# One buffer pool for the weights of an attention stack, and weight splits that wait for DVE's low parts

## The chip, the cores and the metric

The kernel runs on one core of a Trainium2 chip. The metric is device time of one launch in microseconds, the median of several runs. Profiles come from one execution that the hardware profiler recorded.

## The reference

Two transformer-like layers over 2 × 1024 rows of 512 (a residual stream `x`), all float32. Layer 0 adds to `x` a single-head attention of width 128 and a mixing of four streams of 128 columns, whose 4 × 4 matrix per row comes out of 50 Sinkhorn steps. Layer 1 adds a causal attention and an expert layer:

```python
q = (hidden_states @ Wq.T).reshape(b, s, H, D)          # H = 32 heads, D = 128
k = (k_cmp @ Wk_up.T).reshape(b, s, HK, D)              # HK = 8, from a latent of 256 + 256
v = (v_cmp @ Wv_up.T).reshape(b, s, HK, D)
attn = softmax(where(causal, q @ k.T * scale, -1e9))
out = (attn @ v) @ Wo.T                                 # plus a gated LoRA feed-forward of 8 experts
```

Both layers work on a layer-normed `x`. Layer 1 is 2 batches of 1024 rows, and each has 8 groups of four heads that share a key and a value head.

## The kernel before

**Precision.** Every matmul is made of three passes on float16 pairs: a value is split into a high part and a low part (the rest), and high × high, high × low and low × high are summed. So every operand has to be split, by ScalarE (high) and VectorE (low) for results, by GpSimd for weights: `split_pool` is three GpSimd instructions on 128 × 512 (L94 scales in place, L95 writes the high part, L96 subtracts for the low part).

**Layer 1 attention (`layer1_attn`)** walks 16 groups (2 batches of 8) and in each 32 slots. In slot `s` of a group, `row_step` makes one row block: 32 query rows of four heads (128 partitions) against 32·(s+1) keys. PE computes the scores (L88, tile `s`); DVE takes the row minimum of the negated scores with the mask (L282, L286); ACT the exponential (L290) and, one slot later, the scaled high part (`rows_hi`, L307); DVE the low part (`rows_lo`, L313); SP's queue transposes both by DMA to `PT` (L318). A width that is no multiple of 128 is padded with zeros by a GpSimd memset (L317). `last_row` holds the last row minimum recorded so far.

Around the rows other work is recorded at fixed slots by `at(g, s, f)`: attention times values (`av`, L343) from slot `4c + 2k + 5`, output projections (`wo_block`, its result added by DVE at L729) from `4c + 10`, query projections of the next group from 18 or 19, keys and values of the next group (`kv`) from slot 1. Weights are fetched on GpSimd's queue (`fetch`, L677, into the four `f2k` buffers) and then split by `parts_of`. The slots before:

- key and value weights of group g+1: fetched at slot 1, split at 3 (at the end of a batch 17 and 19)
- query weights: fetched at 5, 9, 13, 17, split at 7, 11, 15, 19
- output weights: fetched at 33, 35, 37, 39, split at 35, 37, 39, 41, which are slots 1 to 9 of the next group

**Buffers.** Key and value weights go to a pool `h2k` of three buffers, output weights to `wo` of five, query weights to `wq` of four; all are 2 KB per partition. `h2k` and `wo` also take the normed tiles on their way to the transposed `xT` (`normed_T`), the tiles of the second batch's gate (`tile_of`) and latent weights (`lat_w`).

**Order.** Each engine's queue is in order. The order of each is made when the program is built: a list scheduler places instructions by modelled times and the dependencies that were recorded. `behind(i, j)` adds a dependency without a semaphore: i is placed after j in the modelled order, and nothing waits at run time. In `parts_of` the first instruction of a split is put behind `last_row` in this way. `tc.issue_after(i)` orders the instructions of a block that run on i's engine behind i.

**Other work in the groups.** Recorded at slots of the first eight groups: the Sinkhorn steps of the second batch (`chain_step`, DVE reciprocals L542 and L547 between GpSimd sums L537 to L545), the mixing (`mix0_units`, GpSimd L629), gates, a second layer norm, expert weights (`ffn_w`, which calls `split_pool` directly into `cmp`), and the latent weights.

Of the kernel before, what the change touches and what calls it, by code (L numbers as in the profile page):

```python
# [9 lines left out]
F16 = mybir.dt.float16  # L10
# [6 lines left out]
P = 128  # L17
S = 1024
NB = 2
NT = S // P  # L20
H = 512
NC = H // P
# [3 lines left out]
CAPACITY = 768.0  # L26
LN_EPS = 1e-5
RMS_EPS = 1.1920929e-07
FB, HB, PB, LB, XB, WB = 4, 3, 3, 3, 4, 5
QR = 32  # L30
NR = P // QR
LG = ((0, 1, 2, 3), (4, 5, 6, 7))
# [19 lines left out]
def tile_model(ctx: ExitStack, tc: tile.TileContext, out: bass.AP, a: dict):  # L52
# [11 lines left out]
    def T(tag, shape, dt=F32, bufs=None):  # L64
        count[0] += 1
        kw = {} if bufs is None else {"bufs": bufs}
        return sb.tile(shape, dt, tag=tag, name=f"{tag}_{count[0]}", **kw)

    def C(name, shape, dt=F32):
        return const.tile(shape, dt, tag=name, name=name)  # L70
# [109 lines left out]


    last_pool, last_row, last_T = [None], [None], [None]
    last_hi, last_lo = [None], [None]

    def after(*insts):

# [2 lines left out]
            st.enter_context(tc.issue_after(i.ins))  # L189
        return st  # L190

    def behind(i, j):

        tc.add_manual_dep(i.ins, j.ins.name, mybir.DependencyInfo(
            mybir.DependencyClass.NoSync, mybir.DependencyReason.DATA), reason="behind")

    def rsqrt(y, ve, tag):

# [24 lines left out]
        return V.scalar_tensor_tensor(rs[:, 1, sl], mv[:, sl, 0], -1.0, rs[:, 2, sl],  # L223
                                      ALU.mult, ALU.mult)

    def normed_T(b, mv, rs, t, dst, pool, tags=(("f2k", FB), ("h2k", HB))):

        xn = T(tags[0][0], [P, NC, P], bufs=tags[0][1])
        xf = xn.rearrange("p c d -> p (c d)")
        hl = T(tags[1][0], [P, NC, 2, P], F16, bufs=tags[1][1])  # L230
        if pool > 1:
            A.activation(xf, acc[b, t], AF.Identity, scale=rs[:, 2, t:t + 1], bias=rs[:, 1, t:t + 1])
        elif pool:
            G.tensor_scalar(xf, acc[b, t], rs[:, 2, t:t + 1], rs[:, 1, t:t + 1], ALU.mult, ALU.add)
        else:
            V.tensor_scalar(xf, acc[b, t], rs[:, 2, t:t + 1], rs[:, 1, t:t + 1], ALU.mult, ALU.add)
        last_hi[0] = A.activation(hl[:, :, 0, :], xn, AF.Copy)
        eng = G if pool in (1, 2) else V
        lo = eng.tensor_tensor(hl[:, :, 1, :], xn, hl[:, :, 0, :], ALU.subtract)
        (last_pool if eng is G else last_lo)[0] = lo  # L240
        last_T[0] = nc.sync.dma_start_transpose(dst, hl.rearrange("p c l d -> p (c l d)"))
# [67 lines left out]
    def rows_lo(Pm, r, W, pool, hl, dst):  # L309
        if pool:  # L310
            G.tensor_tensor(hl[:, 1, :W], Pm[:, :W], hl[:, 0, :W], ALU.subtract)
        else:
            lo = V.scalar_tensor_tensor(hl[:, 1, :W], Pm[:, :W], r[:, 1:2], hl[:, 0, :W],  # L313
                                        ALU.mult, ALU.subtract)
        if W < hl.shape[2]:

            behind(G.memset(hl[:, :, W:], 0.0), lo)  # L317
        nc.sync.dma_start_transpose(dst, hl.rearrange("p l k -> p (l k)"))  # L318
# [32 lines left out]
    def front0(b, between=lambda: None):  # L351
        mv, rs = layernorm(b, "a")
        xT = T("xT", [P, NT, 2 * NC, P], F16, bufs=1)
        for ts in F0[b]:
            layernorm_tiles(b, mv, rs, ts)
            for t in ts:
                if b == 0:
                    tags = ("wq", 4), (("h2k", HB), ("wo", WB))[t % 2]
                    normed_T(b, mv, rs, t, xT[:, t], FP[b][t], tags)
                    if t == X1:  # L360
                        with tc.issue_after(last_T[0].ins):
                            load_x(1)
                else:
                    normed_T(b, mv, rs, t, xT[:, t], FP[b][t])
                    between()
            if b == 0 and ts[0] == 0:
                split_w0a()
        lead = [x[0] for x in (last_pool, last_hi, last_lo)]

        ms = T("rms", [P, NT], bufs=2)  # L370
        V.tensor_tensor(ms, rs[:, 0], rs[:, 0], ALU.mult)
        V.tensor_tensor(ms, ms, mv[:, :, 1], ALU.mult)
        V.tensor_scalar(ms, ms, RMS_EPS, None, ALU.add)
        rf = T("rf", [P, NT], bufs=2)
        rsqrt(rf, ms, "rs")
        V.tensor_scalar(rf, rf, 1.0 / 1024.0, None, ALU.mult)
        lg = C(f"lg{b}", [P, NT, 24])
        Vh = T("V", [P, NT, 2, P], F16, bufs=2)
        for t in range(NT):
            p = PP() if t % 2 or b else srow()  # L380
            mm3(p[:, :152], [(lambda l, c=c: xT[:, t, 2 * c + l, :],
                              lambda r, c=c: wv0[:, c, r, :]) for c in range(NC)])
            V.scalar_tensor_tensor(lg[:, t, :], p[:, 128:152], rf[:, t:t + 1], base24,
                                   ALU.mult, ALU.add)
            if CV[b]:
                vf = T("y", [P, P], bufs=1)
                A.activation(vf, p[:, 0:128], AF.Copy)
                A.activation(Vh[:, t, 0, :], vf, AF.Copy)
                G.tensor_tensor(Vh[:, t, 1, :], vf, Vh[:, t, 0, :], ALU.subtract)
            else:  # L390
                evac(p[:, 0:128], Vh[:, t, 0, :], Vh[:, t, 1, :], 1.0)
            between()
        logit[b] = lg

        hh = C(f"hh{b}", [P, NT, 2, 4])
        l4 = lg[:, :, 16:24].rearrange("p t (k n) -> p t k n", k=2)
        mx = T("hmx", [P, NT, 2], bufs=1)
        V.tensor_reduce(mx, l4, AX.X, ALU.max)
        V.tensor_tensor(hh, l4, bc(mx, 3, 4), ALU.subtract)
        A.activation(hh, hh, AF.Exp)  # L400
        V.tensor_reduce(mx, hh, AX.X, ALU.add)
        V.reciprocal(mx, mx)
        V.tensor_tensor(hh, hh, bc(mx, 3, 4), ALU.mult)

        V.tensor_scalar(hh[:, :, 1, :], hh[:, :, 1, :], 1.0 / 128.0, None, ALU.mult)
        if b == 0:
            with after(*lead):
                split_w0b()
        Q = T("Q", [P, 2, S], F16, bufs=2)
        K = T("K", [P, 2, S], F16, bufs=2)  # L410
        for half in range(2):
            sl = slice(512 * half, 512 * half + 512)
            for k, dst in ((0, Q), (1, K)):
                p = proj_T(lambda c, l: wqk0[:, c, l, k * P:(k + 1) * P], xT, half)
                if CQ[b]:
                    qf = T("f2k", [P, 512], bufs=FB)
                    A.activation(qf, p, AF.Identity, bias=bqkv[:, k:k + 1])
                    A.activation(dst[:, 0, sl], qf, AF.Copy)
                    G.tensor_tensor(dst[:, 1, sl], qf, dst[:, 0, sl], ALU.subtract)
                    continue  # L420
                A.activation(dst[:, 0, sl], p, AF.Identity, bias=bqkv[:, k:k + 1])
                V.scalar_tensor_tensor(dst[:, 1, sl], p, bqkv[:, k:k + 1],
                                       dst[:, 0, sl], ALU.add, ALU.subtract)
        return Q, K, Vh, xT, hh, rs
# [243 lines left out]
    def lat_w(mc):  # L668
        st = T("f2k", [P, NC, P], bufs=FB)
        nc.gpsimd.dma_start(st, a["Wlat"][mc])  # L670
        w1 = T("h2k", [P, 2, NC, P], F16, bufs=HB)
        split_pool(st, w1[:, 0], w1[:, 1], 32.0)
        return w1

# [4 lines left out]

    def parts_of(st, tag, scale, bufs):  # L680

        hl = T(tag, [P, 2, 512], F16, bufs=bufs)
        behind(split_pool(st, hl[:, 0], hl[:, 1], scale), last_row[0])
        return hl

    def kv(b, g):
# [4 lines left out]
            got["st"] = fetch(a["Wup"][g])  # L691

        def split():
            w = parts_of(got["st"], *(("h2k", 32.0, HB) if g + b else ("wo", 32.0, WB)))
            got["w"] = w.rearrange("p l (s c d) -> p l s c d", s=2, c=2)
            got["K"] = T("K", [P, 2, S], F16, bufs=2)
            got["V"] = T("V", [P, 2, NT, P], F16, bufs=2)
# [60 lines left out]
    def layer1_attn(kv0, start, extra):  # L758
# [5 lines left out]
        def at(g, s, f):  # L764
            g, s = g + s // NS, s % NS
            fill.setdefault((g, s), []).append(f)
# [29 lines left out]
        for g in range(N):  # L796
            if g + 1 < N:
# [8 lines left out]
                for u in range(4):  # L806
                    at(g, QNN + 2 * u if new else QN + 4 * u, lambda g=g, u=u: q_unit(g + 1, u))
                for hh in range(4):
                    at(g, 33 + 2 * hh, lambda g=g, hh=hh: fetch_wo(g + 1, hh))
                    at(g, 35 + 2 * hh, lambda g=g, hh=hh: split_wo(g + 1, hh))  # L810
            for u in range(4):
                at(g, QH + (1 if (g + 1) % NG == 0 else 3) * u, lambda g=g, u=u: q_unit(g, 4 + u))
            for c in range(NT):
# [174 lines left out]
        xT1[b] = T("xT", [P, NT, 2 * NC, P], F16, bufs=1)  # L988

    def xT_tile(b, t, pool):  # L990
        normed_T(b, *ln1[b], t, xT1[b][:, t], pool, (("f2k", FB), ("h2k", HB)) if b else
                 (("xr", XB), (("h2k", HB), ("wo", WB))[t % 2]))

    def tile_of(b, t):
        d = T("h2k", [P, 2 * NC, P], F16, bufs=HB)
        normed_T(b, *ln1[b], t, d, True, (("f2k", FB), ("xr", XB)))
        return d

# [36 lines left out]
        extra.setdefault((s // (S // QR), s % (S // QR)), []).append(f)  # L1035

    def chain_step():
        with tc.issue_after(last_row[0].ins):
            next(chain, None)

    for k in range(102):
# [93 lines left out]
```

## Time and profile before

| | |
|---|---|
| Median of 3 runs | 1868.62 us (1867.13 to 1870.87) |
| Profiled execution | 1873.71 us |
| Its span | 1871.6 us |
| Granted TensorE clock, mean | 0.971 |
| VectorE busy | 1473.9 us (79%) |
| GpSimd busy | 900.4 us (48%) |
| DMA | 230.25 MB, mean 123 GB/s |

PE is TensorE, PEld its weight loads, DVE VectorE, ACT ScalarE, POOL GpSimd, SP SyncE. Busy times are per engine, so they overlap. Layer 0 ends at about 234 us; a group of layer 1 takes about 92 us. In a row such as `out<-in`, the names are the program's tiles. Idle time in brackets behind an instruction is its engine's, with what ended it.

### The profile page before, as it was taken

What the parts mean: (1) busy time and instruction counts of PE and PEld (TensorE: products, weight loads), DVE (VectorE), ACT (ScalarE), POOL (GpSimd) and SP (SyncE); (2) the same over time, 40 slices, a digit from 0 to 9 for tenths busy, and PEclk for the clock granted to TensorE, in tenths of its full rate; (3) what the DMA queues carried; (4) which work ended last, traced back from release to release, by engine and by line L of the source; (5) the groups of instructions that cost most, each with busy time, mean ns of one, the idle gap of its engine ahead of it and who ended that gap; (6) DMA issues with size and microseconds to landing.
All of it is one profiled execution on the core that took longest, in us unless ns stands there. A gap on an engine that the chain in (4) does not pass through costs nothing. (4 is left out here: it accounts for less than half of the span.)

```text
span 1871.6 us, 34948 instructions
## 1 busy us (share of the span) xinstructions
PE 1724.0 (92%) x11458; PEld 1047.7 (56%) x11458; DVE 1473.9 (79%) x4050; ACT 1198.8 (64%) x2917; POOL 900.4 (48%) x1540
## 2 busy tenths in 40 slices
PE   4756399989999999999999999999999999999998
PEld 3333145656666566566555556566666666655665
DVE  8888977988888878787967767777777878777675
ACT  4747665657666787867535646666676767675554
POOL 5657667576857373727525332334242415155200
PEclk9887699999999999999999999999999999999999
DMA  7425234656554656477538645756565666666456
GB/s 209 91 46 112 76 66 96 149 113 133 129 127 104 150 121 152 99 146 159 134 85 154 124 101 128 131 125 146 115 143 123 137 123 141 118 143 138 89 125 119
DMA packets 707305, 230.25 MB, mean 123 GB/s; under 512 B 689953, under 2 KB 690081, under 8 KB 707122
## 3 DMA queue, kind: packets, MB, share of 16 engines
q1 hardware_dynamic: 691666, 180.75, 47.2%
q0 software_dynamic: 13152, 43.07, 8.6%
q10 hardware_dynamic: 2304, 4.20, 0.7%
q8 instruction: 90, 1.47, 0.3%
q14 instruction: 93, 0.76, 0.1%
HBM read 52.81 MB, written 4.19 MB: 30 GB/s over the span
## 5 line engine op out<-in xcount | busy, mean ns | idle before, releaser
L290 ACT ACTIVATE P<-P,nm 128x1024 f32<-128x1024 f32 (+31 forms) x528 | 391.7, 742 | 261.3 <-DVE nm L282 248.3
L313 DVE SCALAR_TENSOR_TENSOR Phl<-P,r,Phl 128x1024 f16<-128x1024 f32 (+31 forms) x515 | 464.5, 913 | 109.5 <-ACT Phl L307 104.6
L343 PE MATMUL av<-PT,V 128*128 128x256 f16 x3648 | 451.9, 275 | 18.3 <-DMA PT<-Phl 12.7
L88 PE MATMUL s<-K,Q 128*128 128x512 f16 (+22 forms) x2400 | 447.3, 319 | 22.0 <-DVE P L286 16.0
L343 PEld LDWEIGHTS <-V 128*128 128x128 f16 x3648 | 357.6, 99 | 110.4 <-issue 11.6
L307 ACT ACTIVATE Phl<-P,r 128x1024 f16<-128x1024 f32 (+31 forms) x515 | 370.2, 732 | 28.7 <-DMA PT<-Phl 12.6
L88 PE MATMUL pp<-wo,ao 128*128 128x512 f16 x1536 | 373.7, 380 | 4.6 <-ACT ao L104 3.7
L88 PE MATMUL pp<-xT,wq 128*128 128x512 f16 x1536 | 369.3, 380 | 0.9 <-DVE xr L855 0.5
L317 POOL MEMSET Phl<- 128x192 f16 (+2 forms) x384 | 75.8, 207 | 530.5 <-DMA PT<-Phl 414.1
L88 PEld LDWEIGHTS <-Q 128*128 128x128 f16 x2400 | 224.0, 99 | 180.6 <-issue 34.1
L88 PEld LDWEIGHTS <-wq 128*128 128x128 f16 x1536 | 149.6, 98 | 167.5 <-issue 3.0
L88 PEld LDWEIGHTS <-ao 128*128 128x128 f16 x1536 | 149.6, 98 | 155.6 <-ACT ao L104 5.6
L282 DVE CUSTOM_DVE_ANT_0 P<-s,mask,nm 128x272 f32<-128x272 f32 (+15 forms) x256 | 157.4, 616 | 21.2 <-PE s L88 13.3
L286 DVE TENSOR_SCALAR_CACHE_REDUCE P<-s 128x512 f32<-128x512 f32 (+15 forms) x272 | 152.4, 561 | 14.6 <-PE s L88 11.4
L302 ACT ACTIVATE r<-r 128x1 f32<-128x1 f32 x528 | 96.4, 193 | 76.2 <-DVE r L301 76.0
L104 ACT ACTIVATE ao<-av 128x512 f16<-128x512 f32 x128 | 75.4, 589 | 107.2 <-PE av L343 104.0
L301 DVE RECIPROCAL r<-r 128x1 f32<-128x1 f32 x528 | 80.7, 157 | 77.4 <-ACT P L290 73.2
L94 POOL TENSOR_SCALAR f2k<-f2k 128x512 f32<-128x512 f32 x164 | 110.3, 679 | 48.3 <-DMA f2k<-in_Wq 19.3
L729 DVE SCALAR_TENSOR_TENSOR acc<-pp,acc 128x512 f32<-128x512 f32 x128 | 86.8, 678 | 38.3 <-PE pp L88 37.9
L105 DVE SCALAR_TENSOR_TENSOR Q<-pp,Q 128x512 f16<-128x512 f32 x128 | 87.2, 681 | 31.9 <-ACT Q L104 31.8
L282 DVE CUSTOM_DVE_ANT_0 P<-s,mask 128x32 f32<-128x32 f32 (+15 forms) x256 | 104.9, 429 | 8.7 <-PE s L88 8.3
L104 ACT ACTIVATE Q<-pp 128x512 f16<-128x512 f32 x128 | 74.5, 582 | 55.1 <-PE pp L88 53.4
(262 smaller groups left out, 2113.5 us busy)
## 6 DMA issues: line engine op xcount, KB each, us to landing
f2k<-in_Wq POOLq DMA_DIRECT2D x64, 256.0 KB, 3.2
f2k<-in_WoT POOLq DMA_DIRECT2D x64, 256.0 KB, 3.3
PT<-Phl SPq DMA_TRANSPOSE x528, 3.4
acc<-in_x SPq DMA_DIRECT2D x16, 256.0 KB, 4.0
f2k<-in_Wup POOLq DMA_DIRECT2D x16, 256.0 KB, 3.6
out<-acc ACTq DMA_DIRECT2D x16, 256.0 KB, 3.7
xr<-in_x SPq DMA_DIRECT2D x12, 256.0 KB, 3.0
f2k<-in_Wlat POOLq DMA_DIRECT2D x8, 256.0 KB, 5.5
```

The source lines that it names most:

```text
L88: nc.tensor.matmul(dst, lhs(l), rhs(r), start=(i == 0 and j == 0), stop=(i == n - 1 and j == 2))
L94: first = G.tensor_scalar(stage, stage, scale, 1.0, ALU.mult, ALU.mult)
L104: A.activation(hl_hi, src, AF.Copy, scale=scale)
L105: return V.scalar_tensor_tensor(hl_lo, src, scale, hl_hi, ALU.mult, ALU.subtract)
L282: last_row[0] = V.tensor_tensor_reduce(Pm[:, o:o + w], pt[:, :w], mask[:, 512 - w:], -scale, first, ALU.add, ALU.min, nm[:, k:k + 1])
L286: last_row[0] = V.tensor_scalar(Pm[:, o:o + w], pt[:, :w], -scale, first, ALU.mult, ALU.min, accum_out=nm[:, k:k + 1])
L290: A.activation(Pm[:, :W], Pm[:, :W], AF.Exp, bias=last, scale=-1.0, accum_out=r[:, 0:1])
L302: A.activation(r[:, 1:2], r[:, 1:2], AF.Copy, scale=PSCALE)
L307: A.activation(hl[:, 0, :W], Pm[:, :W], AF.Copy, scale=r[:, 1:2])
L313: lo = V.scalar_tensor_tensor(hl[:, 1, :W], Pm[:, :W], r[:, 1:2], hl[:, 0, :W], ALU.mult, ALU.subtract)
L343: nc.tensor.matmul(p, Vh(j, l), PT(r * nj + j), start=(j == 0 and k == 0), stop=(j == nj - 1 and k == 2))
L729: V.scalar_tensor_tensor(acc[b, t], p, 1.0 / 256.0, acc[b, t], ALU.mult, ALU.add)
```

## The change

`h2k` is dropped: its users and those of `wo` share one pool `wo` of nine buffers. The logits of layer 0 move from one constant buffer per batch to one buffer for both. `behind` can make a dependency with a semaphore, and `parts_of` uses it: a split now waits at run time for `last_low`, the last low part (L313) that is recorded. The four output weights of group g+1 are split at slots 22, 25, 28, 31 of group g (26, 28, 30, 32 at the end of a batch), each fetched two slots earlier. The Sinkhorn steps of the second batch are put behind `last_low` instead of `last_row`, without a semaphore.

```diff
-FB, HB, PB, LB, XB, WB = 4, 3, 3, 3, 4, 5
+FB, PB, LB, XB, WB = 4, 3, 3, 4, 9
...
-    last_hi, last_lo = [None], [None]
+    last_hi, last_lo, last_low = [None], [None], [None]
...
-    def behind(i, j):
+    def behind(i, j, wait=False):
+        kind = mybir.DependencyClass.Sync if wait else mybir.DependencyClass.NoSync
         tc.add_manual_dep(i.ins, j.ins.name, mybir.DependencyInfo(
-            mybir.DependencyClass.NoSync, mybir.DependencyReason.DATA), reason="behind")
+            kind, mybir.DependencyReason.DATA), reason="behind")
...
             lo = V.scalar_tensor_tensor(hl[:, 1, :W], Pm[:, :W], r[:, 1:2], hl[:, 0, :W],
                                         ALU.mult, ALU.subtract)
+            last_low[0] = lo
...
-        lg = C(f"lg{b}", [P, NT, 24])
+        lg = T("lg", [P, NT, 24], bufs=1)
...
     def parts_of(st, tag, scale, bufs):
         hl = T(tag, [P, 2, 512], F16, bufs=bufs)
-        behind(split_pool(st, hl[:, 0], hl[:, 1], scale), last_row[0])
+        behind(split_pool(st, hl[:, 0], hl[:, 1], scale), last_low[0] or last_row[0], True)
...
-            w = parts_of(got["st"], *(("h2k", 32.0, HB) if g + b else ("wo", 32.0, WB)))
+            w = parts_of(got["st"], "wo", 32.0, WB)
...
                 for hh in range(4):
-                    at(g, 33 + 2 * hh, lambda g=g, hh=hh: fetch_wo(g + 1, hh))
-                    at(g, 35 + 2 * hh, lambda g=g, hh=hh: split_wo(g + 1, hh))
+                    s = 26 + 2 * hh if new else 22 + 3 * hh
+                    at(g, s - 2, lambda g=g, hh=hh: fetch_wo(g + 1, hh))
+                    at(g, s, lambda g=g, hh=hh: split_wo(g + 1, hh))
...
     def chain_step():
-        with tc.issue_after(last_row[0].ins):
+        with tc.issue_after(last_low[0].ins):
             next(chain, None)
```

The rest of the diff renames `h2k` to `wo` in `normed_T`, `front0`, `lat_w`, `xT_tile` and `tile_of`.

More of the change, by code (lines that the diff above doesn't have):

```diff
@@ L224, in layernorm_tiles, with normed_T @@
                                       ALU.mult, ALU.mult)
-    def normed_T(b, mv, rs, t, dst, pool, tags=(("f2k", FB), ("h2k", HB))):
+    def normed_T(b, mv, rs, t, dst, pool, tags=(("f2k", FB), ("wo", WB))):
         xn = T(tags[0][0], [P, NC, P], bufs=tags[0][1])
@@ L357, in front0 @@
                 if b == 0:
-                    tags = ("wq", 4), (("h2k", HB), ("wo", WB))[t % 2]
+                    tags = ("wq", 4), ("wo", WB)
                     normed_T(b, mv, rs, t, xT[:, t], FP[b][t], tags)
@@ L670, in lat_w @@
         nc.gpsimd.dma_start(st, a["Wlat"][mc])
-        w1 = T("h2k", [P, 2, NC, P], F16, bufs=HB)
+        w1 = T("wo", [P, 2, NC, P], F16, bufs=WB)
         split_pool(st, w1[:, 0], w1[:, 1], 32.0)
@@ L990, in xT_tile @@
     def xT_tile(b, t, pool):
-        normed_T(b, *ln1[b], t, xT1[b][:, t], pool, (("f2k", FB), ("h2k", HB)) if b else
-                 (("xr", XB), (("h2k", HB), ("wo", WB))[t % 2]))
+        normed_T(b, *ln1[b], t, xT1[b][:, t], pool, (("f2k", FB), ("wo", WB)) if b else
+                 (("xr", XB), ("wo", WB)))
     def tile_of(b, t):
-        d = T("h2k", [P, 2 * NC, P], F16, bufs=HB)
+        d = T("wo", [P, 2 * NC, P], F16, bufs=WB)
         normed_T(b, *ln1[b], t, d, True, (("f2k", FB), ("xr", XB)))
```

## The prediction

> **What bounds the kernel now.** I read the engine totals and the 40 slices of the page first.
>
> ```profile
> PE 1724.0 (92%) x11458; PEld 1047.7 (56%) x11458; DVE 1473.9 (79%) x4050; ACT 1198.8 (64%) x2917; POOL 900.4 (48%) x1540
> ...
> PE   4756399989999999999999999999999999999998
> ```
>
> TensorE is the bound from slice 6 on (the two attentions of layer 1), and not in layer 0, its first 234 us. So time can come back only where PE is idle inside the groups. Busy time by windows of one group (92 us), columns PE, PEld, DVE, ACT, POOL, granted clock, DMA:
>
> ```profile
> 347.00:439.00 92.00, 85.95 (x566) 52.59 (x564) 82.22 (x235) 57.41 (x141) 62.95 (x135) 0.98 0.57 124
> 439.00:531.00 92.00, 92.00 (x615) 57.10 (x614) 77.23 (x220) 62.80 (x152) 67.28 (x150) 1.00 0.57 130
> ...
> 702.00:794.00 92.00, 88.87 (x573) 53.80 (x572) 73.04 (x189) 72.72 (x197) 49.98 (x74) 0.98 0.55 123
> ...
> 886.00:978.00 92.00, 84.98 (x577) 50.07 (x576) 74.92 (x211) 42.36 (x100) 36.39 (x58) 0.96 0.50 114
> ...
> 1346.00:1438.00 92.00, 92.00 (x617) 57.22 (x615) 70.08 (x191) 61.58 (x148) 32.59 (x60) 1.00 0.63 130
> ```
>
> Some groups are full (92.00 of 92.00) and cannot be shortened by moving POOL work; others lose 3 to 7 us, with the clock at 0.96 to 0.98. Over all windows from 255 us to the end PE is idle 42.4 us of 1616: the ceiling of any gain, apart from the clock. What makes the gaps? The timeline of the longest one in group 1 (start, us, engine, line):
>
> ```profile
> 387.46 0.98 POOL L95 TENSOR_SCALAR wo<-f2k 128x512 f16<-128x512 f32 x1
> ...
> 388.16 4.70 DVE L313 SCALAR_TENSOR_TENSOR Phl<-P,r,Phl 128x416 f16<-128x416 f32 x1
> ...
> 388.62 1.15 POOL L96 TENSOR_TENSOR wo<-f2k,wo 128x512 f16<-128x512 f32 x1
> ...
> 389.75 0.61 POOL L95 TENSOR_SCALAR wo<-f2k 128x512 f16<-128x512 f32 x1
> 390.33 0.40 POOL L537 TENSOR_TENSOR sk<-sk,sk 128x128 f32<-128x128 f32 x1
> 390.70 1.14 POOL L96 TENSOR_TENSOR wo<-f2k,wo 128x512 f16<-128x512 f32 x1
> ...
> 392.85 0.67 DVE L729 SCALAR_TENSOR_TENSOR acc<-pp,acc 128x512 f32<-128x512 f32 x1
> ...
> 393.57 0.72 PE L88 MATMUL pp<-h2k,cmp 128*128 128x128 f16 x10 [3.58 <-DVE acc L729]
> ...
> 394.62 0.67 DVE L313 SCALAR_TENSOR_TENSOR Phl<-P,r,Phl 128x448 f16<-128x448 f32 x1
> ```
>
> The low part of 416 columns took 4.70 us; the wider one of 448, 6 us later, took 0.67. In between POOL ran two interleaved weight splits without a break. DVE then stored its block late, and PE waited 3.58 us for a PSUM buffer. In the groups by form (busy us, mean ns) a 416-wide low part costs as much on average as an 800-wide one:
>
> ```profile
> L313 DVE SCALAR_TENSOR_TENSOR Phl<-P,r,Phl 128x800 f16<-128x800 f32 x16 | 16.7, 1041 | 2.5 <-ACT Phl L307 2.3
> L313 DVE SCALAR_TENSOR_TENSOR Phl<-P,r,Phl 128x416 f16<-128x416 f32 x16 | 16.5, 1032 | 6.1 <-ACT Phl L307 6.0
> ```
>
> Why the splits come in clusters is in the waits (us in total, times, longest):
>
> ```profile
> POOL wo L95 <- PE pp L88: 87.3, 10, 19.6
> ```
>
> With five wo buffers, a split of output weights stands at the head of POOL's queue until PE has finished with the old ones; then several run on end.
>
> **The change, part by part.**
>
> *Nine buffers in one pool.* After it, four weights of group g, four of g+1 and one key and value weight (4 + 4 + 1) fit. The L95 wait goes; POOL is not the bound, so the 87.3 us are worth nothing by themselves. What is late next on POOL is the new wait below. In layer 0 the normed tiles take these buffers too; ACT's waits there for a transpose to free an h2k buffer were 2.0 us in all (2 times), while the longest stretch there, 187 to 234 us, has DVE busy 44.3 of 46.8 us. I take 0, bounds −2 to +2. The logits' new buffer adds no instruction: 0.
>
> *The four output-weight splits move* from slots 33..39 (1..7 of the next group) to 22..31 (26..32 at the batch's end): per split one DMA issue on POOL's queue (about 0.57 us of it, 256 KB, 3.3 us to landing), and L94, L95, L96 at 0.62 + 0.62 + 1.16 = 2.4 us. SP's queue gets nothing. The fetch is two slots (2 × 92/32 = 5.8 us) ahead of its split, so the 3.3 us are covered. They leave the stretch where key, value and first query splits begin, so two splits hardly meet: in the changed program's POOL order each split of groups 0 to 6 and 9 to 15 is a triple L94, L95, L96 of its own, with the pad memsets in row order between; only at the change of batch, where the latent and expert weights join, are splits still interleaved. Before, almost every group had six or more on end.
>
> *The splits wait for the low part of the row before.* A split then starts when DVE has just finished a low part and has 2.4 us until it reaches the next, if DVE's queue holds that much. By DVE's order in the changed program (groups 10 to 14; an evacuation of 512 columns 0.68 us, a minimum about 0.6) six of nine splits meet no low part; slot 3 meets the three short ones of 128 to 192 columns, slots 22 and 25 one each. So collisions do not vanish, but they are capped: one split at most, 2.4 us, where the run above cost 4.70 − 0.65 = 4 us.
>
> What this should remove, by PE's gaps and the POOL rows before each:
> - 393.6 us: 3.58, and 0.46 just behind: 4.0
> - 677.4 us (two wo splits on a 448-wide low part of 1.67 us): 0.9
> - 780.7 us (2.10; half the POOL work there is L629, which is not governed): 1.0
> - 887.8 us (1.60; half is L239): 0.8
> - 1132.3 us (1.91, behind a 256-wide low part of 3.47 us): 1.9
>
> Sum 8.6. The clock: 0.98 over 92 us is 1.8 us; group 1 gets it back whole, group 5 half: 2.7. [...]
>
> Not touched: the gap of 3.91 us at 912 (splits of the expert layer's weights, which do not pass through the changed helper), those at 1012 to 1037 (latent weights, whose buffers only get more), 615 (L629 on the low part), 3.1 us at 1723, layer 0, the tail.
>
> *What the wait costs.* Behind a waiting split on POOL stand pad memsets, Sinkhorn sums, weight fetches and L629. A pad memset delayed by the wait delays its row's transpose, whose reader on PE comes three to four slots later, 9 to 12 us; the transpose lands after 3.4. So 5 to 8 us of cover; without it each split could cost PE its 2.4 us, 9 splits in 9 early groups some 190 us at the far end, which nothing in the trace is near, since POOL already sits 19.6 us at once in the old wait without a PE gap of that size. Below zero is not excluded either (shorter low parts in full groups give DVE slack). I take +2 us: one gap like that at 617 us (1.3, a late PT) or two.
>
> [...]
>
> *Sinkhorn steps* (98 reciprocals of 0.35 us on DVE) now stand behind the low part instead of the row's minimum. In DVE's order the last lies after the 117th low part, before after the 118th: 0.
>
> Sum: −8.6 − 2.7 + 2 = −9.3 us on the profiled run's 1873.7 (span 1871.6), and the same on the median of 1868.6, 5 us below that run: 1859.
>
> **Rivals.** About 0.2% (3.7 us) is what a measurement of this kernel can tell from no change.
> - *Slower: the wait makes POOL late.* In the early groups (0 to 8) POOL is 50 to 67 us busy of 92, and splits wait on low parts that come in bunches. If memsets and fetches slip past the cover, PE waits for PT or a weight. It decides from 11.3 / 15 = 0.75 us per group on; at one gap of 1.3 us (as at 617 us) in each of 15 groups it is 19.5 against 11.3 gained, +8: 1877. For it: PT waits of PE do exist (12.7 us, 10 times). Against: POOL's order keeps rows in order.
> - *The gaps only move:* DVE is 73 to 82 of 92 us busy in those groups, so another late DVE result takes over: 1867.
> - *More goes:* the clusters were behind the gaps at 615, 912 and 1012 to 1037 too, by delays handed on; six tenths of the 42.4 us go, 25: 1843.
> - *It does nothing,* because the scheduler placed the splits there already: excluded by the POOL orders, which differ.
>
> **How the numbers follow.** Forecast (−4 to −16 us) 0.51; more goes 0.18; gaps only move 0.11; slower 0.20. Faster 0.69, same 0.11, slower 0.20. Likeliest 1859, its own range 1853 to 1865; the range for 8 in 10 reaches from 1842, half of the case in which more goes, to 1876, the nearer half of the slower one.
>
> **What would show it.** Right: L95's wait on PE gone; no low part over 3 us beside L94 to L96; the gaps at 393, 677, 1132 gone; group 1 near 92.0 busy at 1.00. Wrong: new POOL waits on L313 followed by PE waits for PT or wo; low parts as long as before; or layer 0 longer, which I hold constant.

## The result and the profile after

The changed kernel takes 1865.08 us (median of 14 runs, 1861.5 to 1867.17), the kernel before 1869.22 us (median of 14 runs, 1867.04 to 1876.18): ratio 0.9971, 95% interval [0.9958, 0.9983], which is 5.4 us of 1869. The profiled execution took 1866.04 us with a span of 1864.3; before it was 1873.71 and 1871.6.

The waits of POOL in the changed kernel (us in total, times, longest):

```profile
POOL f2k L94 <- DVE Phl L314: 433.1, 90, 28.4
POOL Phl L319 <- DMA PT<-Phl: 97.7, 26, 11.1
```

The wait of L95 on PE (87.3 us before) is gone. In its place POOL stands 433.1 us in the new wait on the low part, and the waits of the pad memsets have shrunk from 414.1 to 97.7: POOL idles as long as before, in another place.

The low parts by form in the changed kernel (busy us, mean ns of one | idle before):

```profile
L314 DVE SCALAR_TENSOR_TENSOR Phl<-P,r,Phl 128x800 f16<-128x800 f32 x16 | 16.8, 1050 | 1.1 <-ACT Phl L308 1.0
...
L314 DVE SCALAR_TENSOR_TENSOR Phl<-P,r,Phl 128x416 f16<-128x416 f32 x16 | 10.8, 677 | 0.5 <-ACT Phl L308 0.5
```

The 416-wide one costs 677 ns where it cost 1032, and the 800-wide one 1050 where it cost 1041. Instruction and shape are the same; what ran beside it is not. All 512 low parts of layer 1 together have 41.0 us above their undisturbed cost, where they had 75.9 (excess over 210 ns + 1.045 ns per column, a line through the undisturbed rows: 0.65 us for 416, 1.05 for 800). I call this sum the excess from here on. Nearly all of it lies in low parts beside which POOL ran something: the 207 with no POOL instruction beside them before, and the 278 after, hold 0.6 us of it each time. The longest low part is now 3.04 us, before 4.70.

Busy time by windows of one group after (PE, PEld, DVE, ACT, POOL, granted clock, DMA):

```profile
347.00:439.00 92.00, 87.07 (x588) 54.61 (x587) 79.99 (x240) 57.40 (x143) 66.66 (x149) 1.00 0.60 122
439.00:531.00 92.00, 89.21 (x584) 54.79 (x582) 72.44 (x212) 58.72 (x147) 60.30 (x137) 0.98 0.60 126
...
702.00:794.00 92.00, 91.77 (x612) 56.80 (x611) 72.28 (x195) 76.08 (x204) 49.13 (x74) 1.00 0.59 127
...
886.00:978.00 92.00, 81.74 (x509) 47.78 (x508) 76.69 (x216) 45.36 (x114) 36.68 (x64) 0.91 0.48 106
```

Some windows gained (702 to 794: 88.87 became 91.77, clock 0.98 became 1.00). The window 439 to 531, which was full, now idles for 2.8 us, and the one at 886, around the change of batch, lost 3.2 us more and runs at 0.91 instead of 0.96. Over the 16 windows from 255 to 1713 us PE's idle time fell only from 34.1 to 31.1 us.

The longest new gap in group 1, by the timeline (start, us, engine, line):

```profile
383.53 0.66 POOL L94 TENSOR_SCALAR f2k<-f2k 128x512 f32<-128x512 f32 x1
...
385.20 1.15 POOL L96 TENSOR_TENSOR wq<-f2k,wq 128x512 f16<-128x512 f32 x1
385.27 0.35 DVE L544 RECIPROCAL sk<-sk 128x32 f32<-128x32 f32 x1 [1.56 <-POOL sk L541]
...
386.35 0.64 DVE L314 SCALAR_TENSOR_TENSOR Phl<-P,r,Phl 128x416 f16<-128x416 f32 x1
...
386.91 0.68 DVE L732 SCALAR_TENSOR_TENSOR acc<-pp,acc 128x512 f32<-128x512 f32 x1
387.64 0.59 PE L88 MATMUL pp<-xT,wq 128*128 128x512 f16 x2 [3.02 <-DVE acc L732]
```

The 416-wide low part is quick now (0.64). But DVE stood 1.56 us at the head of its queue in a Sinkhorn reciprocal, because POOL was late with the sum: a weight split lay between the Sinkhorn sums. So the store of the output block (L732) came late all the same, and PE waited 3.02 us where it had waited 3.58.

Where the span goes, from the starts of the groups (first scores of slot 0), in us:

| profiled run | until group 0 | groups 0–5 | groups 6–7 (change of batch) | groups 8–14 | rest |
|---|---|---|---|---|---|
| before | 265.2 | 574.0 | 258.5 | 650.2 | 123.6 |
| after | 262.0 | 566.1 | 262.8 | 649.1 | 124.3 |

The groups 0 to 5 won 7.9 us and the change of batch gave 4.3 back. The first column is scatter for the most part: over the runs below with the nine-buffer pool, which differ in layer 1 alone, it lies between 259.9 and 266.2 us. Differences of single profiled runs under some 4 us (my estimate from this range) I do not take for effects by themselves.

### The profile page after: what moved, and what is told of

The parts are those of the page before. It is cut to its first block, busy times and chain, and to the rows that moved or that the text cites. A ratio compares the mean times of both kernels' runs of the same rounds, so it can differ in the third digit from the quotient of the medians.

```text
span 1864.3 us, 35096 instructions
## 1 busy us (share of the span) xinstructions
PE 1723.1 (92%) x11458; PEld 1047.2 (56%) x11458; DVE 1448.0 (78%) x4050; ACT 1194.4 (64%) x2917; POOL 895.1 (48%) x1540
## 4 chain that ended last, share of the span: by engine, by line
PE 46%; DVE 3%; DMA 2%; POOL 1%; issue 1%; ACT 1%; ACTq 0%; DVEq 0%; POOLq 0%
PE pp L88 25%; PE av L345 11%; PE s L88 10%; DMA PT<-Phl 1%; DVE Phl L314 1%; DMA f2k<-in_loraB 1%; DVE f2k L881 0%; POOL cmp L96 0%; DVE P L287 0%; ACT Phl L308 0%; DVE P L283 0%; DMA f2k<-in_Wq 0%; POOL wo L240 0%; DVE ao L105 0%; POOL cmp L95 0%
## 5 line engine op out<-in xcount | busy, mean ns | idle before, releaser
L314 DVE SCALAR_TENSOR_TENSOR Phl<-P,r,Phl 128x1024 f16<-128x1024 f32 (+31 forms) x515 | 429.8, 845 | 88.5 <-ACT Phl L308 79.2
L88 PE MATMUL pp<-xT,wq 128*128 128x512 f16 x1536 | 373.1, 380 | 5.0 <-DVE acc L732 4.1
L94 POOL TENSOR_SCALAR f2k<-f2k 128x512 f32<-128x512 f32 x164 | 105.9, 647 | 522.4 <-DVE Phl L314 433.1
L287 DVE TENSOR_SCALAR_CACHE_REDUCE P<-s 128x512 f32<-128x512 f32 (+15 forms) x272 | 152.7, 563 | 22.4 <-PE s L88 20.2
L283 DVE CUSTOM_DVE_ANT_0 P<-s,mask,nm 128x272 f32<-128x272 f32 (+15 forms) x256 | 157.4, 616 | 12.8 <-PE s L88 5.2
L319 POOL MEMSET Phl<- 128x192 f16 (+2 forms) x384 | 72.3, 210 | 134.7 <-DMA PT<-Phl 97.7
L283 DVE CUSTOM_DVE_ANT_0 P<-s,mask 128x32 f32<-128x32 f32 (+15 forms) x256 | 104.6, 433 | 29.6 <-PE s L88 29.1
L732 DVE SCALAR_TENSOR_TENSOR acc<-pp,acc 128x512 f32<-128x512 f32 x128 | 87.5, 683 | 47.2 <-PE pp L88 46.7
L105 DVE SCALAR_TENSOR_TENSOR Q<-pp,Q 128x512 f16<-128x512 f32 x128 | 87.3, 682 | 35.7 <-ACT Q L104 35.5
```

What stands on the lines that cost most here:

```text
L88: nc.tensor.matmul(dst, lhs(l), rhs(r), start=(i == 0 and j == 0), stop=(i == n - 1 and j == 2))
L94: first = G.tensor_scalar(stage, stage, scale, 1.0, ALU.mult, ALU.mult)
L105: return V.scalar_tensor_tensor(hl_lo, src, scale, hl_hi, ALU.mult, ALU.subtract)
L283: last_row[0] = V.tensor_tensor_reduce(Pm[:, o:o + w], pt[:, :w], mask[:, 512 - w:], -scale, first, ALU.add, ALU.min, nm[:, k:k + 1])
L287: last_row[0] = V.tensor_scalar(Pm[:, o:o + w], pt[:, :w], -scale, first, ALU.mult, ALU.min, accum_out=nm[:, k:k + 1])
L732: V.scalar_tensor_tensor(acc[b, t], p, 1.0 / 256.0, acc[b, t], ALU.mult, ALU.add)
```

## The experiments

Each ratio is to the kernel before, run beside it on the same chip. That kernel's own median was 1872.92 us beside four of the experiments (nine buffers alone; pool and slots; without the semaphore; the wait on the row minimum) and 1869.2 to 1869.9 beside the others, so between these two sets a difference of 0.2% in the ratio says little. Line numbers are those of the changed kernel, in which L313 has become L314, L317 L319, L318 L320, L282 L283, L286 L287, L542 L544 and L729 L732.

An edit here seldom changes one thing alone, since the list scheduler places the work around it anew. Between the kernel before and the changed one some 2000 of DVE's 4050 instructions stand elsewhere in its order, and between most of the pairs compared below 600 to 1800. Only spreading (of the expert weights' splits, and of the latent ones) leaves the order nearly as it was, with 20 to 100 of 4050. So the price of any other edit is that of the edit and of the new order together.

**Each part by itself.** *Nine buffers alone*: the kernel before with `h2k` merged into nine `wo` buffers and the shared logits buffer; old slots, no wait.

```diff
-FB, HB, PB, LB, XB, WB = 4, 3, 3, 3, 4, 5
+FB, PB, LB, XB, WB = 4, 3, 3, 4, 9
```

> The kernel before with one thing of the change: the pool of nine buffers (and the shared logits buffer); slots, order and missing wait as before. Theory (the gain comes from splits that no longer run on end and start behind a low part): POOL's L95 wait for PE (87 us) goes, but clusters of splits stay, low parts keep some 65 to 76 us of excess; time within 3 us of before. Rival (the pool is what pays, because POOL no longer stands in front of PE's buffers): 4 to 5 us faster than before. Layer 0's 3 us come from the pool in either case, if they are real: first scores of group 0 at 262 instead of 265 us.

Measured: 1888.36 us, 1.0078 [1.0051, 1.0106]: slower by 14.6 us, where the theory had no more than 3 us and the rival a gain. The excess rose to 90.9 us. The timeline shows a cluster that the kernel before did not have:

```profile
756.99 6.51 DVE L314 SCALAR_TENSOR_TENSOR Phl<-P,r,Phl 128x224 f16<-128x224 f32 x1 [0.78 <-ACT Phl L308]
757.34 0.62 POOL L95 TENSOR_SCALAR wo<-f2k 128x512 f16<-128x512 f32 x1
757.92 0.61 POOL L94 TENSOR_SCALAR f2k<-f2k 128x512 f32<-128x512 f32 x1
758.50 0.61 POOL L95 TENSOR_SCALAR wq<-f2k 128x512 f16<-128x512 f32 x1
759.09 1.15 POOL L96 TENSOR_TENSOR wo<-f2k,wo 128x512 f16<-128x512 f32 x1
```

A 224-wide low part (0.44 us undisturbed) takes 6.51 us while POOL runs three interleaved splits. PE's wait right behind it is 1.14 us. Of the loss, 16.4 us lie in groups 6 and 7 and 4.0 in groups 0 to 5; groups 8 to 14 won 4.7. In groups 6 and 7 a second low part of that kind (6.03 us at 983 us) stands before a PE gap of 3.73 us; the longest gap there, 6.55 us at 1042 us, is a wait for the transpose of a normed tile (`xT`), and what made that late was not tried.

*Eight buffers* instead of nine, else the same:

```diff
-FB, PB, LB, XB, WB = 4, 3, 3, 4, 9
+FB, PB, LB, XB, WB = 4, 3, 3, 4, 8
```

> The kernel before with one pool of eight buffers instead of three and five (old slots, no wait), one fewer than in the run with nine, which gave 1.0078. Theory: nine were slower because POOL's waits on PE, which had spaced the splits, are gone; with eight one buffer is short (4 + 4 + 1), some of these waits stay (over 30 us), and the time lies between: 1.002 to 1.006. Rival: the loss comes from sharing one pool, which mixes the two kinds of weights in one order whatever the number: 1.008 again.

Measured: 1872.52 us, 1.0013 [0.9997, 1.0028], excess 84.5 us. That is below the theory's range (from 1.002) and not to be told from 1; the rival's 1.008 is excluded. So sharing one pool costs nothing that could be told; the ninth buffer does. The wait of the output weights' L95 on PE was 87.3 us in the kernel before, 43.0 here, and with nine buffers one wait of 13.8:

```profile
POOL wo L95 <- PE pp L88: 43.0, 10, 9.3
```

The excess rises as this wait falls (75.9, 84.5, 90.9 us), and the largest step in time comes with the last buffer. This fits the theory that the wait, which looked worthless, had kept splits apart; it does not show it, as the order of instructions changed too.

*Everything but the pool*: the changed kernel with `h2k` of three and `wo` of five buffers.

```diff
-FB, PB, LB, XB, WB = 4, 3, 3, 4, 9
+FB, HB, PB, LB, XB, WB = 4, 3, 3, 3, 4, 5
```

> The changed kernel with the old pools: three h2k and five wo buffers; new slots, wait and Sinkhorn edit as in the change. Theory: the slots carry the gain and need the ninth buffer, because with five wo buffers a split in mid-group has to wait until PE has used up the old weights, so that POOL stands in L95 waiting on PE again (more than 87 us in all), the splits run in a row afterwards, and the time is at or above that of the kernel before: ratio 1.00 to 1.01. Rival: mid-group slots are enough without the pool, since a split that is late is still covered by the ten slots until its weight is used: 0.997, as the change.

Measured: 1877.57 us, 1.0049 [1.0028, 1.007]. The time is as the theory had it; the wait on PE is back, with 45.9 us, half of the 87 that I expected. The slots need the larger pool. The excess is 65.3 us, less than the 75.9 of the kernel before, and yet the time is longer: the excess tells how much low parts are held up, and not by itself what PE loses.

*Everything but the slots*: the changed kernel with the output weights split at 35 to 41 again.

```diff
-                    s = 26 + 2 * hh if new else 22 + 3 * hh
-                    at(g, s - 2, lambda g=g, hh=hh: fetch_wo(g + 1, hh))
-                    at(g, s, lambda g=g, hh=hh: split_wo(g + 1, hh))
+                    at(g, 33 + 2 * hh, lambda g=g, hh=hh: fetch_wo(g + 1, hh))
+                    at(g, 35 + 2 * hh, lambda g=g, hh=hh: split_wo(g + 1, hh))
```

> The changed kernel with the output weights' splits back at slots 35 to 41; pool, wait and Sinkhorn edit stay. Theory (the slots carry the gain, since without them nothing spaces the splits, and the pool takes away the PE wait that did): slower than before, 1.004 to 1.010, near the pool alone (1.0078), long low parts of 4 us and more again. Rival (the wait would space them in any slot): 0.997 to 1.0.

Measured: 1884.97 us, 1.0088 [1.0062, 1.0113], excess 94.9 us. The run-time wait does not rescue the old slots. Its timeline has the longest low part of all runs:

```profile
879.58 9.16 DVE L314 SCALAR_TENSOR_TENSOR Phl<-P,r,Phl 128x480 f16<-128x480 f32 x1 [0.72 <-ACT r L303]
879.95 1.15 POOL L96 TENSOR_TENSOR wo<-f2k,wo 128x512 f16<-128x512 f32 x1
881.08 0.61 POOL L95 TENSOR_SCALAR wq<-f2k 128x512 f16<-128x512 f32 x1
...
881.77 1.51 POOL L235 TENSOR_SCALAR f2k<-acc,rsb 128x512 f32<-128x512 f32 x2
...
883.25 1.14 POOL L96 TENSOR_TENSOR wq<-f2k,wq 128x512 f16<-128x512 f32 x1
884.36 3.36 POOL L240 TENSOR_TENSOR xr<-f2k,xr 128x512 f16<-128x512 f32 x3
...
889.39 0.24 PE L88 MATMUL pp<-gw,wo 128*128 128x32 f16 x3 [7.78 <-DVE Q L105]
```

POOL has no pause until 887.7, where a fetch follows; the low part ends 1.0 us after that. PE waits 7.78 us for what DVE has behind it. Of POOL's work in that stretch some 5 us are L235 and L240, the normed tiles of the second batch's gate, and only 3 us are splits: the splits are not all that ran beside the low part. Only the slots of four splits per group were edited against the changed kernel. In the changed kernel groups 0 to 5 take 566.1 us, here 587.9. In groups 8 to 14, most of which are full, the excess falls as well by the slots, from 37.8 to 10.5 us, but their time does not (648.0 us here, 649.1 in the changed kernel).

**The wait.** *Pool and slots, no wait*: `behind` without a semaphore on `last_row`, as before, and the Sinkhorn steps behind `last_row`.

```diff
-        behind(split_pool(st, hl[:, 0], hl[:, 1], scale), last_low[0] or last_row[0], True)
+        behind(split_pool(st, hl[:, 0], hl[:, 1], scale), last_row[0])
...
-        with tc.issue_after(last_low[0].ins):
+        with tc.issue_after(last_row[0].ins):
```

> Pool of nine and the output weights' splits in mid-group, no wait, order behind the row minimum as before, Sinkhorn steps too. Theory: each split is a triple of its own, so no low part over 3 us beside them, but a split may start anywhere: low parts sum to about 445 us (before 464, changed 430), a third to a half of the gain, 2 to 3 us. Rival (the wait alone pays): no gain over the pool alone. Rival (the slots alone pay): all 4 to 5 us.

Measured: 1863.97 us, 0.9956 [0.9939, 0.9974], excess 50.1 us. Pool and slots by themselves give 0.44%, as much as the whole change within the noise (1863.97 against 1865.08 us): the rival "the slots alone pay" held.

*The changed kernel without the semaphore* (order behind `last_low` kept):

```diff
-        behind(split_pool(st, hl[:, 0], hl[:, 1], scale), last_low[0] or last_row[0], True)
+        behind(split_pool(st, hl[:, 0], hl[:, 1], scale), last_low[0] or last_row[0])
```

> The changed kernel with the splits ordered behind the low part without a semaphore, so they don't wait at run time. Theory: they start early, beside a low part: low parts sum to 440 to 455 us, 2 to 3 us slower than the changed kernel. Rival (the wait costs as much as it brings): as fast or 1 to 3 us faster than the changed kernel, and the new gap at 467 us behind a late PT goes.

Measured: 1870.85 us, 0.9991 [0.9973, 1.0008], excess 59.4 us: the wait at run time may be worth some 0.2%, but the intervals overlap (0.9971 [0.9958, 0.9983] with it).

*The wait on the row minimum* instead of the low part:

```diff
-        behind(split_pool(st, hl[:, 0], hl[:, 1], scale), last_low[0] or last_row[0], True)
+        behind(split_pool(st, hl[:, 0], hl[:, 1], scale), last_row[0], True)
```

> The changed kernel with its wait on the row minimum recorded last instead of the low part: as many waits at the same slots, but a split now starts about when a low part is next. Theory (it is the place in DVE's queue that counts): low parts rise to 445 us or more, 2 to 4 us slower than the changed kernel. Rival (any wait that spaces the splits does): the same time as the changed kernel within 1 us and low parts near 430.

Measured: 1870.09 us, 0.9986 [0.997, 1.0003], excess 60.7 us. A wait on the earlier event is no better than none, as the theory had it (what counts is that the split starts behind a low part). But against 0.9971 the intervals overlap here as well, so these two runs leave it open. The pair further down shows that wait and place together pay; which of the two does is not shown.

**The Sinkhorn steps.** The changed kernel with only that edit undone:

```diff
-        with tc.issue_after(last_low[0].ins):
+        with tc.issue_after(last_row[0].ins):
```

> The changed kernel with the Sinkhorn steps back behind the row minimum; pool, slots and the wait stay. From the runs so far the slots give most (0.9956 without wait and without the Sinkhorn edit, against 0.9971 with all). Theory A (the Sinkhorn edit costs, since its reciprocals then hold DVE's queue for late POOL sums, as before the 3.0 us gap at 387 us): 0.995 or better, groups 0 to 2 shorter by 3 us or more, that gap gone. Theory B (the wait costs as much as it brings and the Sinkhorn edit is free): 0.997 as the changed kernel, the same group times within 2 us.

Measured: 1855.87 us, 0.9927 [0.9902, 0.9953]; the interval lies wholly below that of the changed kernel. The edit costs 0.44%, 8 us. Its excess is 35.5 us, no low part takes over 1.84 us, the gap at 387 us is gone, and at the change of batch PE is slightly busier at a better clock (81.74 at 0.91 in the changed kernel):

```profile
886.00:978.00 92.00, 82.81 (x541) 48.82 (x540) 75.33 (x218) 47.09 (x117) 33.23 (x56) 0.98 0.45 106
```

By groups the gain hardly lies where the steps run. They end at 590 us (595 in the changed kernel). Groups 0 to 2 are 4.2 us shorter, as theory A had it, but groups 3 to 5 are 3.7 longer, so that groups 0 to 5 take 565.7 us here and 566.1 there. Groups 6 and 7 take 252.8 against 262.8. So most of the cost lies behind the steps, and there the two programs differ only in the order that the list scheduler gave: one edit of an early dependency shifts its modelled times, and the instruction order differs on all five engines. Which of the reordered instructions make the change of batch slower was not tried and stays open.

**Splits that the change left alone.** One gap late in the changed kernel answers to the 3.1 us at 1723 that the prediction left alone:

```profile
1714.94 2.29 PE L345 MATMUL av<-PT,V 128*128 128x256 f16 x10 [3.38 <-DMA PT<-Phl]
```

In front of it POOL runs the expert weights' splits (`cmp`, 1696 to 1709 us) with few pauses, and beside them a low part of 704 columns takes 2.92 us (0.95 undisturbed). *Spread*: each of the six splits gets a slot of its own with the wait, once per batch (slots are counted over all groups).

```diff
-            split_pool(st, w[:, k, 0], w[:, k, 1], scale)
+                behind(split_pool(stg[k], w[:, k, 0], w[:, k, 1], scale), last_low[0], True)
...
-    put(0, FW, ffn_w)
-    put(58, 2, ffn_w)
+    ffn_at(FW, (212, 213, 215, 216, 218, 219))
+    ffn_at(466, (467, 468, 469, 471, 472, 474))
```

> The changed kernel with the expert weights' six splits, until now recorded in one place twice, spread over slots 212 to 219 and 467 to 474 with the same wait behind a low part. Theory (clusters of splits make the gaps, wherever they are): the 3.4 us gap at 1714 us goes, low parts fall below 425 us, and the group of the second half where the clock is 0.91 (886 to 978 us) loses less than its 10.3 us: 3 to 8 us faster than the changed kernel, 0.993 to 0.9955 of before. Rival (that group is bound by its extra DVE work, the clusters only lie beside it): within 2 us of the changed kernel.

Measured: 1857.84 us, 0.9935 [0.9912, 0.9957]. The gap at 1714 is gone: group 14 takes 91.8 us instead of 98.1. Groups 8 to 14 take 642.8 us, 6.3 less than in the changed kernel. The other place where the theory looked for a gain gave little: from 886 to 978 us PE still idles 10.2 us (10.3 before the edit), though at a clock of 0.96 instead of 0.91. As the order is nearly unchanged here, this is the cleanest of the tests. The same edit was made twice more, in versions that follow, again with the order nearly kept. By the medians it gave 7.2 us here, 3.0 us with the Sinkhorn edit undone (1855.87 and 1852.87), and nothing on pool and slots without the wait on attention weights (1863.97 and 1863.73).

**Together.** *Sinkhorn steps back, expert splits spread*: the changed kernel with the diff of the Sinkhorn experiment and that of the spread one.

> The changed kernel with the Sinkhorn steps back behind the row minimum and the expert weights' splits spread over slots, each behind a low part. Alone the two edits gave 0.9927 and 0.9935 against 0.9971 of the change. Theory: they act at different places (the Sinkhorn steps in groups 1, 5 and 6, the expert splits in groups 7 and 15), so their gains of 0.44% and 0.36% add: 0.989, some 1849 us. Rival: both only loosen the same POOL queue around the change of batch, so the second adds little: 0.992 to 0.993, 1855 us.

Measured: 1852.87 us (median of 6 runs) against 1869.88, 0.9907 [0.9888, 0.9927]. That lies between the theory (the gains add: 0.989) and the rival (0.992 to 0.993), and the interval reaches both, so how far the two add is open. This is the best version found but for the last one of this section, which equals it, and it beats the changed kernel (0.9971 [0.9958, 0.9983]) with intervals apart. By groups: 565.1 in 0 to 5, 254.1 in 6 and 7, 642.8 in 8 to 14. The largest waits of PE that are left from 255 us on are at the change of batch and on ACT:

```profile
PE pp L88 <- DMA xT<-wo: 5.6, 1, 5.6
PE pp L88 <- ACT ao L104: 4.8, 6, 1.7
```

*The same without the wait on attention weights*:

```diff
-        behind(split_pool(st, hl[:, 0], hl[:, 1], scale), last_low[0] or last_row[0], True)
+        behind(split_pool(st, hl[:, 0], hl[:, 1], scale), last_row[0])
```

> As the kernel with both edits, but the splits of attention weights stand behind the row minimum in the modelled order alone, as before the change, and wait for nothing at run time (the expert splits keep their wait). Theory: the run-time wait is worth 0.3%, as between the two versions with the Sinkhorn steps behind the row minimum (0.9956 without, 0.9927 with it): 0.992 here, with the low parts' excess some 15 us above. Rival: slots alone do it, and the wait was worth something only where expert or Sinkhorn work crowded the queue: within 0.001 of the kernel with both edits.

Measured: 1863.73 us, 0.9968 [0.9955, 0.9981], excess 49.5 us against 33.7. The wait, with its place behind the low part, is worth 0.6% here, twice what was expected, and now the intervals are apart. In the profiled runs 2.1 of the difference lies in groups 0 to 5 and 5.7 in groups 6 and 7. This pair differs both in the semaphore and in what the split is ordered behind, and with that in the order of much other work.

*The latent weights' splits spread too*, four slots with the wait:

```diff
-        split_pool(st, w1[:, 0], w1[:, 1], 32.0)
+        behind(split_pool(st, w1[:, 0], w1[:, 1], 32.0), last_low[0], True)
...
-        put(0, LA + 2 * mc - 4, lambda mc=mc: lw.update({mc: lat_w(mc)}))
+        put(0, (233, 237, 240, 242)[mc], lambda mc=mc: lw.update({mc: lat_w(mc)}))
```

> As the kernel with both edits, and the four splits of latent weights at slots 233, 237, 240, 242 (counted over all groups) each behind a low part with a wait. They stand beside the gaps of PE at 1012 to 1037 us, some 4 us in all. Theory: the gaps come from splits in a cluster on the low parts, as everywhere else: these gaps shrink by half, 2 us or 0.1% less than the kernel with both edits. Rival: the gaps there come from the change of batch itself (fewer matmuls ready, rows of 32 to 128 columns): no difference.

Measured: 1851.9 us, 0.9906 [0.9887, 0.9925]: no difference, as the rival said; but the theory's 0.1% would have been too small to tell. The excess falls by 2.5 us, but PE still waits beside these splits, for DMA transposes of a row and of a normed tile (`PT` at 1006 us, `xT` at 1013).

## Why the prediction was right, and where its steps were not

The forecast was −9.3 us; the ratio says −5.4, the profiled runs −7.7. The time of 1865.1 us lies at the upper edge of the forecast's own range (1853 to 1865). Direction and order of size held, and so did the mechanism of the main term. The sum did not hold term by term: two terms that I set to nothing were each larger than the result.

*Clusters of splits starve DVE's low parts, and isolating them brings time back.* Right: the four slots alone move the excess from 94.9 to 41.0 us and the ratio from 1.0088 to 0.9971, though with a new order of DVE's work; and where the order hardly changed, spreading the expert splits took the gap behind them away. "No low part over 3 us beside L94 to L96" was just missed (3.04 us, beside two L96 at 1032 us). That groups 0 to 6 and 9 to 15 would hold only whole triples was misread: in the trace splits are interleaved with those of the expert weights in groups 6 and 14 too, and in 14 the gap at 1715 us stands behind them.

*Nine buffers: 0, bounds −2 to +2.* Wrong as a term of its own. With the old slots they cost 0.78%; with the new slots, taking them away costs 0.78% (0.9971 to 1.0049). The step that failed is "the 87.3 us are worth nothing by themselves": the wait was idle time of an engine that is not the bound, but the edit that removed it cost 14.6 us. That it set when POOL's next work began, and so what that work ran into, is the likely reason; the new order that came along is not excluded. Buffers and slots are one edit; neither has a price alone.

*Gaps, 8.6 us.* Over-counted. The gap at 393 (4.0 of the 8.6) moved to 387 and kept 3.02 us: what the rivals called "the gaps only move" happened there, with a Sinkhorn reciprocal as the next late thing on DVE. Those at 781 (forecast to lose half) and 1132 went, and that at 615 too, which I had called untouched; the one at 1132 had begun 9 us after the long low part that I put it down to, so that reading was loose. Where 0.94 us stood at 677, 1.44 stand at 673; the one at 888 went half (0.75 at 890). The one at 912 (3.91), also called untouched, became four: at 900, 906, 934 and 937 us, of 2.27, 2.25, 1.42 and 2.22, each on a result of DVE, and the window around them is 3.2 us worse. In sum 3.0 us of idle time went from the 16 windows. Group 1 reached 87.07 of 92 us, not the 92.0 that I had named as a sign.

*Clock, 2.7 us.* Wrong in size and sign: by an estimate from the windows' clocks (what each lacks to 1.00, rounded to 0.01, times its 92 us), the loss was 11.0 us before and is 12.0 us after. Group 1 got its 1.8 back, group 5 and the windows from 531 and 978 us too; groups 0 and 2 lost 1.8 each, and the window from 886 us 4.6. With the Sinkhorn edit undone the loss is 3.7 us. In the two windows from 886 to 1070 us that version has 2.2 us less idle time on PE and 6.4 us less loss by the clock, against the 10.0 us by which its groups 6 and 7 are shorter; by this estimate much of its gain is the clock.

*The wait, +2.* Wrong sign, as far as the runs tell. Without it the changed kernel is at 0.9991 (intervals overlap), and in the version with both edits the wait with its place is worth 0.6%. It does cost what I described in one place. The timeline of group 2 in the changed kernel:

```profile
462.97 0.65 POOL L95 TENSOR_SCALAR wo<-f2k 128x512 f16<-128x512 f32 x1
...
464.25 0.20 POOL L319 MEMSET Phl<- 128x128 f16 x1
...
467.57 1.85 PE L345 MATMUL av<-PT,V 128*128 128x256 f16 x9 [2.42 <-DMA PT<-Phl]
```

The pad memset stands behind a split, and the transposed block reaches PE 3.1 us after it. I had counted 5 to 8 us of cover for this; here it was used up. It stayed at one gap of that kind in the early groups, so the rival "the wait makes POOL late" did not come about, although POOL stands 433 us in the wait. (That rival's 50 to 67 busy us of POOL in groups 0 to 8 hold up to group 5; from 886 to 1070 us it is 36.4 and 43.3.)

*Sinkhorn steps, 0.* Wrong by 8 us. I had compared the place of the last step in DVE's order (117th against 118th low part) and concluded that nothing moves. Over the groups 0 to 5 that is about right in sum (566.1 us against 565.7); the loss is in groups 6 and 7, which start more than 200 us after the last of the steps and where only the order of instructions differs. A comparison of both orders over the whole program, not only at the moved steps, would have shown that there was something to price.

By ratios to the kernel before, then: pool with slots −8 us (0.9956), the wait −5 (0.9927, with overlapping intervals), the Sinkhorn edit +8 (0.9971). The forecast had −9.3 for the first two together, where 0.9927 makes −13.6, and 0 for the third. The two misses, −4 and +8 us, have opposite signs and partly cancel: that the total came as near as it did is in part luck.

## What to carry to other kernels

Work on an engine off the critical path still has a place in time (here the edit that removed an 87.3 us wait of such an engine cost 14.6 us): before a buffer is added to remove its wait, ask what that wait keeps apart, and move the released work to where it can run alone in the same edit. Where two engines hinder each other, starting the one right behind the other's instruction by a semaphore can be worth its wait; here that was so with pieces that are short and spread (0.9907 with the wait and its place, 0.9968 without). And where a scheduler makes the order, test each small edit alone, since a changed dependency can cost more far downstream than where it was put (here 10.0 us in groups 6 and 7, and 0.4 in groups 0 to 5).

## What the hardware showed that was not expected

- Low parts of DVE ran on while POOL ran several instructions in succession: one took 4.70 us in the kernel before, one 6.51 with nine buffers, one 9.16 with the old slots, for work of 0.44 to 0.71 us undisturbed. Each was late by 4 us or more; the longest POOL instruction of a split, L96, takes 1.16 us (median in the kernel before). In these three rows the instruction ended within 1.1 us of a break in POOL's run, a fetch or a memset. A break was not always enough (the one of 9.16 us ran on past a memset at 881.64 us, the one of 6.51 past another at 761.89 us), nor always there (in the changed kernel one of 2.92 us at 1702.84 us ended beside an L95, which then took 1.31 us instead of 0.62).
- The longer gap on PE did not come with the lower granted clock: in the changed kernel's 347 to 439 the longest gap is 3.02 us at a clock of 1.00, and in the version with the Sinkhorn steps back the same window has none over 1.69 us and 0.98.
